# Loading x by blocks of 32 rows to 128 partitions instead of by column strips to 32

## The chip, the core and the metric

The kernel runs on one core of a Trainium2 chip. A core has a matrix engine (PE, with its weight loads PEld), a vector engine (DVE), a scalar engine (ACT), a general one (POOL) and SyncE (SP), which here issues nearly all transfers between the device's memory (HBM) and the on-chip memory of 128 partitions (SBUF). The transfers are carried out by sixteen DMA engines. The metric is device time in microseconds (us) of one execution.

## The reference

One graph layer over 128 graphs of 128 nodes with 768 features and 12 heads of 64, all in float32:

```
h = relu(layernorm(x))                     # per node, over 768 features
q, k, v = h @ Wq + bq, h @ Wk + bk, h @ Wv + bv
scores = q k^T / 8 + beta * adj            # per head
scores = where(adj > 0, scores, -9e15)
out = x + softmax(scores) v                # heads put side by side
```

So each graph needs its x twice: once normalized and turned for the products, and once as it is for the last sum.

## The kernel before

The graphs go in 32 groups G of four; a group is two pairs (r = 0, 1) of graphs. The weights stay the same for all groups. The three products q, k and v of a group are done in three slices, `qk0`, `v`, `qk1` (half of the columns of q and k, all of v, the other half). From group 1 on, each slice is a product of a 2 x 3 by a 3 x 3 table of blocks in 15 block products (`PRODUCTS`) instead of 18, and each block product is done in 7 zones instead of 8. The combined weight blocks (T, 128 x 896 values) are made once; eleven stay in SBUF and the other 34 of a group's 45 are kept in HBM and loaded anew for each group (`load_T`, L440) into a ring of five buffers (`RING`). A load of the ring is issued when the product that used the buffer before has ended. The products are `product`, L681: 7 zones by 2 halves, which the profile shows as 28 matmul records.

**x for the products.** The pair tile (`xp[G, r]`, made by `home_x`) holds x in a form of its own: partition a*32 + i, block m = 4g + b, 192 values: graph g of the pair, row 32b + i, features 192a to 192a + 191. There are two such pairs in a group but one buffer for both, so a pair is loaded when the pair before it was turned. ACT normalizes block by block in place (`norm`, L560; eight instructions of 128 x 192 per pair), DVE turns 32 x 32 squares (`to_hT`, L580), three times per pair, into the operands A. The scales and shifts of the norm come by another way: whole rows of x (`load_row`, L513) are summed by ACT, and the few numbers are written to HBM (`turn_out`, L539, "turned<-row") and read back by all partitions (`turn_in`, L543, "block<-turned").

**How x comes.** `load_x` issues a transfer for each a: source 32 rows i, 8 blocks (g, b), 192 values; destination 32 partitions with 8 x 192 values each. The four parts of a pair are issued at four places of the program.

**What sets the order.** In the groups from 1 on the order of all steps is written out: `TABLE` gives each step a time in units of a block product (45 to a group, counted from the group's start), and the steps are put into the program in the order of these times, between the block products. So the engines' queues, SP's among them, are in the order of the table. x of pair 0 is issued two groups ahead, in the `qk1` slice (times about -53 to -49, of which -45 is one group), among the loads of T for the next group's `qk0`; x of pair 1 one group ahead, at the end of `qk0` (times about -33 to -30), among the loads of T for `v`. SP is in order: a transfer that waits holds all behind it. The transfers take turns over eight semaphores, and each waits until the one that last used its semaphore has landed.

SP also loads x once more for the last sum (`load_xo`, L763), the adjacency (`load_adj`, L599) and sends the result (`send`, L908).

Of the kernel before, what the change touches and what calls it, by code (L numbers as in the profile page):

```python
# [20 lines left out]
GRP = 4  # L21
# [10 lines left out]
@with_exitstack  # L32
def kernel(
    ctx: ExitStack,
    tc: tile.TileContext,
    x: bass.AP,
    adj: bass.AP,
    wq: bass.AP,
    bq: bass.AP,
    wk: bass.AP,  # L40
    bk: bass.AP,
    wv: bass.AP,
    bv: bass.AP,
    beta: bass.AP,
    out: bass.AP,
):

    nc = tc.nc
    keep = ctx.enter_context(tc.tile_pool(name="keep", bufs=1))
    bad = keep.tile([1, 1], I32, name="bad")
    args = (x, adj, wq, bq, wk, bk, wv, bv, beta, out)
    direct(tc, *args, bad)
    again = nc.values_load(bad[0:1, 0:1])
    with tc.If(again > 0):
        general(tc, *args)  # L60
# [64 lines left out]
TABLE = (  # L125
    (-103.105, 'row', 0), (-86.74, 'row_stats', 0), (-85.688, 'row', 1), (-78.233, 'row_stats', 1),
    (-76.202, 'row', 2), (-71.584, 'row_stats', 2), (-67.928, 'row', 3), (-64.453, 'row_stats', 3),
    (-54.853, 'moments'), (-53.424, 'load_x', 0, (0,)), (-50.853, 'load_x', 0, (1,)), (-49.522, 'powers'),
    (-51.725, 'load_x', 0, (2,)), (-49.052, 'turn_out'), (-49.398, 'load_x', 0, (3,)), (-46.515, 'turn_in'),
    (-40.942, 'norm', 0, 2, 4), (-41.357, 'norm', 0, 0, 2), (-40.317, 'norm', 1, 2, 4), (-39.199, 'norm', 1, 0, 2),  # L130
    (-37.336, 'turn', 'A01'), (-34.768, 'turn', 'A02'), (-35.86, 'turn', 'A00'), (-33.123, 'load_x', 1, (0,)),
    (-32.146, 'load_x', 1, (1,)), (-30.708, 'load_x', 1, (2,)), (-32.534, 'load_x', 1, (3,)), (-24.763, 'inner', 'A00'),
    (-24.393, 'norm', 2, 0, 2), (-25.315, 'norm', 2, 2, 4), (-23.262, 'norm', 3, 2, 4), (-23.244, 'norm', 3, 0, 2),
    (-23.578, 'inner', 'A01'), (-20.844, 'adj'), (-18.417, 'inner', 'A02'), (-20.599, 'turn', 'A11'),
# [4 lines left out]
    (5.399, 'sum', 'S5'), (8.41, 'sum', 'S14'), (9.857, 'sum', 'S11'), (17.129, 'scores', 0, 2),  # L139
    (17.594, 'mask', 2), (18.011, 'exp', 2), (17.884, 'scores', 0, 1), (20.163, 'mask', 1),  # L140
    (23.187, 'exp', 1), (23.44, 'scores', 0, 0), (24.691, 'mask', 0), (26.808, 'xo', 2),
    (29.787, 'exp', 0), (33.304, 'attend', 2), (34.708, 'drain', 2), (38.169, 'recip', 2),
    (37.453, 'attend', 1), (40.226, 'divide', 2), (40.335, 'xo', 1), (40.001, 'drain', 1),
    (40.047, 'attend', 0), (42.314, 'xo', 0), (41.101, 'drain', 0), (41.291, 'recip', 1),
    (42.019, 'add', 2), (43.363, 'send', 2), (41.655, 'recip', 0), (47.272, 'xo', 5),
    (42.336, 'divide', 0), (46.026, 'divide', 1), (47.4, 'add', 1), (49.422, 'send', 1),
    (47.396, 'scores', 1, 2), (47.912, 'mask', 5), (47.949, 'scores', 1, 0), (49.895, 'add', 0),
    (49.151, 'mask', 3), (51.424, 'send', 0), (50.757, 'exp', 5), (51.214, 'scores', 1, 1),
    (51.428, 'mask', 4), (56.184, 'xo', 4), (50.986, 'exp', 3), (52.741, 'attend', 5),
    (53.334, 'drain', 5), (53.605, 'recip', 5), (54.069, 'divide', 5), (54.524, 'attend', 3),  # L150
    (55.36, 'drain', 3), (57.434, 'recip', 3), (54.287, 'xo', 3), (57.116, 'add', 5),
    (58.808, 'send', 5), (52.838, 'exp', 4), (58.432, 'divide', 3), (57.867, 'attend', 4),
    (58.283, 'drain', 4), (58.872, 'recip', 4), (61.984, 'divide', 4), (63.775, 'add', 3),
    (69.353, 'add', 4), (70.997, 'send', 4), (72.651, 'send', 3),
)
FIRST = (
# [70 lines left out]
def direct(ctx, tc, x, adj, wq, bq, wk, bk, wv, bv, beta, out, bad):  # L227
# [10 lines left out]
    nc = tc.nc  # L238
# [9 lines left out]
    SQ = 32  # L248
    NB = P // SQ
# [12 lines left out]
    xg, xp, A, full, wide, biasT, vt, qk = {}, {}, {}, {}, {}, {}, {}, {}  # L262
# [8 lines left out]
    def flat(lo, hi):  # L271
        return sbig[:, lo:hi]
# [7 lines left out]
    def home_x(G, r):  # L280
        if (G, r) in ((0, 0), (1, 1)):
            t = flat(2 * RAW, 2 * RAW + 2 * D).rearrange("p (m f) -> p m f", f=QD)
        else:
            t = work.tile([P, 2 * NB, QD], F32, tag="x", name=f"x_{G}_{r}", bufs=1)
        xp[G, r] = t
        for g in range(2):
            xg[G, 2 * r + g] = t[:, g * NB:(g + 1) * NB, :]
        return t

    def load_x(G, r, parts=range(NB)):  # L290
        if parts[0] == 0:
            home_x(G, r)
        src = x[G * GRP + 2 * r:G * GRP + 2 * r + 2].rearrange("g (b i) (a f) -> a i (g b) f", i=SQ, a=NB)
        for a in parts:
            nc.sync.dma_start(xp[G, r][a * SQ:(a + 1) * SQ], src[a])


# [144 lines left out]
    raw_qk0(0, (nc.sync, nc.scalar))  # L442
    raw_qk0(1)
    load_x(0, 1)
    raw_qk0(2)
    name_raw(0, qk0_raw)
# [130 lines left out]
    def to_hT(G, r, k):  # L577
        t = home_A(G, f"A{r}{k}")
        src = xp[G, r].rearrange("p m (c j) -> p c m j", c=NC)[:, 2 * k:2 * k + 2]
        return nc.vector.transpose(t.rearrange("p c (m i) -> p c m i", i=SQ), src)  # L580
# [178 lines left out]
    es, xo = {}, {}  # L759
# [432 lines left out]
    def then(at, f, *args):  # L1192
        todo.setdefault(at, []).append(lambda: f(*args))
# [83 lines left out]
    for r in range(2):  # L1277
        then(5, load_x, 1, r)
# [32 lines left out]
        then(n, step, 2 - (n > 8))  # L1311
    sums_at(1, ((12, "S1"), (13, "S9"), (14, "S10"), (15, "S2")))
    then(0, row_moments, 2)
    for a in range(NB):
        then((7 + a, "post"), load_x, 2, 0, (a,))
    then((14, "post"), load_row, 3, 0)
    then(12, homes.append, block(len(SPOT)))
    bias(1, 4, 6, 8)
    for n in range(2, RING):
# [4 lines left out]
        "scores": scores, "scores3": lambda G, u, js: [scores(G, u, j) for j in js], "mask": mask, "exp": expo, "xo": load_xo, "attend": attend, "drain": drain, "recip": recip,  # L1324
        "divide": divide, "add": add, "send": send, "sum": sum_acts, "norm": norm, "inner": inner,
        "turn": lambda G, name: to_hT(G, int(name[1]), int(name[2])), "bias1": bias_turn, "square": bias_square,
        "bias2": bias_mask, "bias3": bias_sum, "load_x": load_x, "row": load_row, "row_stats": row_stats,
        "moments": moments, "powers": powers, "turn_out": turn_out, "turn_in": turn_in, "adj": add_raw,
        "halve": lambda G: halve_bias(), "scores_half": scores_half, "attend_half": attend_first, "out_half": out_half,
    }  # L1330
# [19 lines left out]
    while events:  # L1350
        _, _, f, args = heapq.heappop(events)
# [149 lines left out]
```

## Time and profile before

| | us |
|---|---|
| median of 3 runs | 2677.48 (2674.48 to 2677.64) |
| the profiled execution | 2675.62 |
| its span, first to last instruction | 2673.7 |
| PE busy / DVE / ACT / POOL | 2645.9 / 2165.9 / 1754.7 / 2089.9 |
| HBM read / written | 647.99 MB / 66.05 MB |

A page of the profile gives busy times, the DMA queues, the waits and the chain of work that ended last; a view by window gives each engine's busy time and the mean busy share of the sixteen DMA engines ("DMA share"); a timeline gives instructions in order of time, with the start in us, the duration in us, the engine, the line and "out<-in". "SPq" is SP's queue: the duration there is that of the issue, and "x3" means that rows are merged, with the waits between them. "Landing" is the time from an issue until all of the data is there. A row of waits reads: who waited, for whom, us in total, times, the longest.

### The profile page before, as it was taken

The page shows a single profiled execution, that of the slowest core. Times are in us where ns is not written, and L with a number is a line of the kernel's source. Part 1 is how long each engine was busy: PE and PEld are TensorE (multiplying, and loading weights), DVE is VectorE, ACT ScalarE, POOL GpSimd, SP SyncE. Part 2 cuts the span into 40 slices and gives each one's busy share as a digit, 9 for nine tenths or more (in the row PEclk, how much of TensorE's full clock was granted, in tenths as well). Part 3 has the DMA queues.
Part 4 walks back from the last instruction along what each step waited for, and adds up shares of the span by engine and source line. Part 5 has one row for each costly group of instructions (what it writes and reads, how often), then busy time and mean ns, then how long its engine had stood idle before and what let it go on. Part 6 is the DMA issues. An engine that isn't in the chain of part 4 may idle for free.

```text
span 2673.7 us, 121363 instructions
## 1 busy us (share of the span) xinstructions
PE 2645.9 (99%) x52041; PEld 2565.2 (96%) x52041; DVE 2165.9 (81%) x2702; ACT 1754.7 (66%) x4608; POOL 2089.9 (78%) x3043
## 2 busy tenths in 40 slices
PE   9999999999999999999999999999999999999998
PEld 8799999999999999999999999999999999999997
DVE  7878887878887778888788877888887888778876
ACT  2567766677766677666777666776667776667654
POOL 4877778877778877788777788777887777887774
PEclk9999999999999999999999999999999999999999
DMA  8888888888888988888888888889888888888875
GB/s 247 270 272 270 276 280 272 275 287 262 285 279 272 282 269 271 281 278 269 280 265 283 278 272 267 274 271 285 272 272 280 265 282 280 265 277 275 249 247 165
DMA packets 526964, 721.97 MB, mean 270 GB/s; under 512 B 105932, under 2 KB 370648, under 8 KB 526424
## 3 DMA queue, kind: packets, MB, share of 16 engines
q1 hardware_dynamic: 525776, 713.38, 84.4%
q8 instruction: 411, 6.73, 1.0%
q14 instruction: 129, 1.06, 0.1%
q10 hardware_dynamic: 648, 0.79, 0.1%
HBM read 647.99 MB, written 66.05 MB: 267 GB/s over the span
## 4 chain that ended last, share of the span: by engine, by line
PE 95%; DMA 3%; DVE 1%; issue 0%; SPq 0%; ACT 0%; ACTq 0%; DVEq 0%
PE pair L681 78%; PE pair L776 7%; PE pair L855 6%; PE pair L1048 3%; DMA T_qk<-kept_qk 2%; DMA sbig<-in_L_gnn_Wk_dram 0%; PE pair L1265 0%; DVE home L704 0%; PE pair L1053 0%; DMA x<-in_x_dram 0%; SPq L336 0%; PE pair L926 0%; SPq L908 0%; DVE e L789 0%; DVE st L464 0%
## 5 line engine op out<-in xcount | busy, mean ns | idle before, releaser
L704 DVE TENSOR_TENSOR home<-home,pair 128x896 f32<-128x896 f32 x836 | 880.8, 1077 | 225.5 <-PE pair L681 192.7
L681 PE MATMUL pair<-sbig,T_qk 128*64 128x128 f32 x13020 | 833.0, 274 | 9.2 <-DMA T_qk<-kept_qk 6.9
L681 PEld LDWEIGHTS pair<-sbig,T_qk 128*64 128x64 f32 x13020 | 711.6, 137 | 28.7 <-issue 16.5
L739 POOL TENSOR_TENSOR home<-home 128x256 f32<-128x256 f32 x308 | 263.5, 855 | 339.3 <-DVE home L704 339.0
L681 PE MATMUL pair<-A,T_qk 128*64 128x128 f32 x6944 | 446.0, 273 | 0.3 <-issue 0.3
L855 PE MATMUL pair<-v,e 128*64 128x65 f32 x6048 | 412.6, 221 | 0.7 <-issue 0.7
L681 PE MATMUL pair<-T_v,sbig 128*64 128x128 f32 x6944 | 404.1, 273 | 2.1 <-issue 1.5
L681 PEld LDWEIGHTS pair<-T_v,sbig 128*64 128x64 f32 x6944 | 382.2, 137 | 8.3 <-ACT e L836 5.0
L836 ACT ACTIVATE e<-e,sm 128x64 f32<-128x64 f32 x1512 | 381.7, 341 | 5.0 <-DVE sm L824 3.4
L681 PEld LDWEIGHTS pair<-A,T_qk 128*64 128x64 f32 x6944 | 384.0, 137 | 0.4 <-issue 0.4
L855 PEld LDWEIGHTS pair<-v,e 128*64 128x64 f32 x6048 | 370.7, 137 | 3.8 <-issue 0.8
L724 ACT ACTIVATE home<-pair 128x640 f32<-128x640 f32 x340 | 240.4, 707 | 189.0 <-PE pair L681 187.7
L681 PE MATMUL pair<-sbig,res_qk 128*64 128x128 f32 x4340 | 314.0, 273 | 0.3
L742 POOL TENSOR_TENSOR home<-home 128x256 f32<-128x256 f32 x308 | 264.3, 858 | 24.1
L885 ACT ACTIVATE sm<-pair,tiny 128x8 f32<-128x8 f32 x189 | 50.8, 269 | 338.4 <-PE pair L855 338.4
L789 DVE SCALAR_TENSOR_TENSOR e<-pair,biasT 128x1024 f32<-128x1024 f32 x189 | 229.3, 1213 | 34.1 <-PE pair L776 33.1
L740 POOL TENSOR_TENSOR home<-home 128x256 f32<-128x256 f32 x308 | 230.6, 749 | 24.1
L681 PEld LDWEIGHTS pair<-sbig,res_qk 128*64 128x64 f32 x4340 | 240.5, 137 | 1.4 <-DVE home L704 1.3
L560 ACT ACTIVATE x<-x,block 128x192 f32<-128x192 f32 x480 | 222.6, 540 | 0.0
L726 ACT ACTIVATE home<-pair,bqk 128x128 f32<-128x128 f32 x680 | 214.1, 377 | 0.0
L798 ACT ACTIVATE e<-e 128x1024 f32<-128x1024 f32 x189 | 196.1, 1055 | 20.3 <-DVE e L789 12.7
L741 POOL TENSOR_TENSOR home<-home 128x128 f32<-128x128 f32 x308 | 180.4, 586 | 24.2
(208 smaller groups left out, 4489.9 us busy)
## 6 DMA issues: line engine op xcount, KB each, us to landing
T_qk<-kept_qk SPq DMA_DIRECT2D x713, 448.0 KB, 4.7
T_v<-kept_v SPq DMA_DIRECT2D x341, 448.0 KB, 4.7
xo<-in_x_dram SPq DMA_DIRECT2D x190, 256.0 KB, 5.3
out_dram<-xo SPq DMA_DIRECT2D x189, 256.0 KB, 5.2
x<-in_x_dram SPq DMA_DIRECT2D x248, 192.0 KB, 7.6
sbig<-in_x_dram SPq DMA_DIRECT2D x116, 384.0 KB
kept_qk<-prep_qk SPq DMA_DIRECT2D x23, 448.0 KB, 2.8
adj<-in_adj_dram SPq DMA_DIRECT2D x128, 64.0 KB, 4.1
```

The costliest lines, as they stand in the source:

```text
L560: nc.scalar.activation(t, t, AF.Relu, bias=shift[G, n], scale=rstd[G, n])
L681: nc.tensor.matmul(p[q:q + HD, at, :], lhs[:, q:q + HD], rhs, start=(first and at % 4 == 0), stop=True, skip_group_check=True)
L704: nc.vector.tensor_tensor(t, t, p[:, 0:7], op)
L724: nc.scalar.activation(t[:, 0:5], p[:, 0:5], AF.Copy, scale=float(sign))
L726: nc.scalar.activation(t[:, at], p[:, at], AF.Identity, bias=bqk[:, of, oc:oc + 1], scale=float(sign))
L739: e.tensor_tensor(t[:, 1:4:2], t[:, 1:4:2], twice(5), ALU.add)
L740: e.tensor_tensor(t[:, 2:5:2], t[:, 2:5:2], twice(1), ALU.add)
L742: e.tensor_tensor(t[:, 0:7:6], t[:, 0:7:6], twice(2), ALU.add)
L789: nc.vector.scalar_tensor_tensor(e[:, :, at], ps[:, :, at], SCORE_CAP * ISCALE, bias[:, :, at], op0=ALU.min, op1=ALU.add)
L798: nc.scalar.activation(e, e, AF.Exp, scale=1.0 / ISCALE)
L836: nc.scalar.activation(o[:, r, b, 0:HD], pa[:, r, b, 0:HD], AF.Copy, scale=t[:, 1, r, b:b + 1])
L855: nc.tensor.matmul(pa[q:q + HD, 2 * g + i, :], k[:, q:q + HD], vt[G, "v", r, h // 4][:, 4 * g + h % 4, :], start=True, stop=True, skip_gro ...
```

## The change

The transfers of a pair's x become eight, one for each graph g and block b of 32 rows (`load_piece`, m = 4g + b): source 96 KB of HBM in one piece (32 rows of 768 values), read as 4 strips a, 32 rows i and 192 values; destination block m of all 128 partitions. The table has two pieces at the place of each old part (0.02 and 0.32 behind it, in the order of time). The rest of the table has the same times and is only sorted. The three pairs that are loaded in the opening (pair 1 of group 0 and both of group 1, the last into a buffer of its own) still come by `load_x`. All but SP's queue keep their instructions and their order.

```diff
-    (-54.853, 'moments'), (-53.424, 'load_x', 0, (0,)), (-50.853, 'load_x', 0, (1,)), (-49.522, 'powers'),
+    (-54.853, 'moments'), (-53.404, 'piece', 0, 0), (-53.104, 'piece', 0, 1), (-51.705, 'piece', 0, 2),
...
-    def load_x(G, r, parts=range(NB)):
-        if parts[0] == 0:
+    def load_piece(G, r, m):
+
+        if not m:
             home_x(G, r)
+        g, b = m // NB, m % NB
+        nc.sync.dma_start(xp[G, r][:, m], x[G * GRP + 2 * r + g, b * SQ:(b + 1) * SQ].rearrange("i (a f) -> a i f", a=NB))
+
+    def load_x(G, r):
+        home_x(G, r)
         src = x[G * GRP + 2 * r:G * GRP + 2 * r + 2].rearrange("g (b i) (a f) -> a i (g b) f", i=SQ, a=NB)
-        for a in parts:
+        for a in range(NB):
             nc.sync.dma_start(xp[G, r][a * SQ:(a + 1) * SQ], src[a])
...
-    for a in range(NB):
-        then((7 + a, "post"), load_x, 2, 0, (a,))
+    for m in range(2 * NB):
+        then((7 + m // 2, "post"), load_piece, 2, 0, m)
```

On SP, x of pair 0 of group 9 (the names are tiles with their numbers, then the shape of the destination) stands before the change so:

```order
L295 DMA x_0_9848<-in_x_dram 32x8x192
L440 DMA T_qk_1_9867<-kept_qk_1_366 128x896
L440 DMA T_qk_0_9903<-kept_qk_0_360 128x896
L295 DMA x_0_9848<-in_x_dram 32x8x192 x2
L440 DMA T_qk_5_9943<-kept_qk_5_449 128x896
L763 DMA xo_1_9955<-in_x_dram 128x4x128
L295 DMA x_0_9848<-in_x_dram 32x8x192
L539 DMA turned_9962<-row_9_9957 4x32x8
L763 DMA xo_0_10025<-in_x_dram 128x4x128
```

and behind the change so (the same lines stand 8 further down in the file):

```order
L297 DMA x_0_9904<-in_x_dram 128x1x192 x2
L448 DMA T_qk_1_9924<-kept_qk_1_366 128x896
L448 DMA T_qk_0_9960<-kept_qk_0_360 128x896
L297 DMA x_0_9904<-in_x_dram 128x1x192 x4
L448 DMA T_qk_5_10002<-kept_qk_5_449 128x896
L771 DMA xo_1_10014<-in_x_dram 128x4x128
L297 DMA x_0_9904<-in_x_dram 128x1x192 x2
L547 DMA turned_10022<-row_9_10016 4x32x8
L771 DMA xo_0_10085<-in_x_dram 128x4x128
```

Each part has become two pieces at the same place. At the end of `qk0`, x of pair 1 of group 8 stands among the loads of T for `v`; before the change:

```order
L295 DMA x_1_9199<-in_x_dram 32x8x192 x3
L440 DMA T_v_9251<-kept_v_782 128x896
L513 DMA sbig<-in_x_dram 128x768
L908 DMA out_dram<-xo_5_8890 128x4x128
L440 DMA T_v_9282<-kept_v_743 128x896
L295 DMA x_1_9199<-in_x_dram 32x8x192
L440 DMA T_v_9300<-kept_v_656 128x896
```

and behind it:

```order
L297 DMA x_1_9251<-in_x_dram 128x1x192 x5
L448 DMA T_v_9305<-kept_v_782 128x896
L297 DMA x_1_9251<-in_x_dram 128x1x192
L521 DMA sbig<-in_x_dram 128x768
L916 DMA out_dram<-xo_5_8942 128x4x128
L448 DMA T_v_9337<-kept_v_743 128x896
L297 DMA x_1_9251<-in_x_dram 128x1x192 x2
L448 DMA T_v_9356<-kept_v_656 128x896
```

Here the sixth piece has come behind the first T, ahead of the row and the sent result.

More of the change, by code (lines that the diff above doesn't have):

```diff
@@ L127 @@
     (-76.202, 'row', 2), (-71.584, 'row_stats', 2), (-67.928, 'row', 3), (-64.453, 'row_stats', 3),
-    (-54.853, 'moments'), (-53.424, 'load_x', 0, (0,)), (-50.853, 'load_x', 0, (1,)), (-49.522, 'powers'),
-    (-51.725, 'load_x', 0, (2,)), (-49.052, 'turn_out'), (-49.398, 'load_x', 0, (3,)), (-46.515, 'turn_in'),
-    (-40.942, 'norm', 0, 2, 4), (-41.357, 'norm', 0, 0, 2), (-40.317, 'norm', 1, 2, 4), (-39.199, 'norm', 1, 0, 2),
-    (-37.336, 'turn', 'A01'), (-34.768, 'turn', 'A02'), (-35.86, 'turn', 'A00'), (-33.123, 'load_x', 1, (0,)),
@@ L132 @@
-    (-32.146, 'load_x', 1, (1,)), (-30.708, 'load_x', 1, (2,)), (-32.534, 'load_x', 1, (3,)), (-24.763, 'inner', 'A00'),
-    (-24.393, 'norm', 2, 0, 2), (-25.315, 'norm', 2, 2, 4), (-23.262, 'norm', 3, 2, 4), (-23.244, 'norm', 3, 0, 2),
-    (-23.578, 'inner', 'A01'), (-20.844, 'adj'), (-18.417, 'inner', 'A02'), (-20.599, 'turn', 'A11'),
[3 rows of a table removed]
+    (-54.853, 'moments'), (-53.404, 'piece', 0, 0), (-53.104, 'piece', 0, 1), (-51.705, 'piece', 0, 2),
+    (-51.405, 'piece', 0, 3), (-50.833, 'piece', 0, 4), (-50.533, 'piece', 0, 5), (-49.522, 'powers'),
@@ new lines @@
+    (-49.378, 'piece', 0, 6), (-49.078, 'piece', 0, 7), (-49.052, 'turn_out'), (-46.515, 'turn_in'),
+    (-41.357, 'norm', 0, 0, 2), (-40.942, 'norm', 0, 2, 4), (-40.317, 'norm', 1, 2, 4), (-39.199, 'norm', 1, 0, 2),
+    (-37.336, 'turn', 'A01'), (-35.86, 'turn', 'A00'), (-34.768, 'turn', 'A02'), (-33.103, 'piece', 1, 0),
+    (-32.803, 'piece', 1, 1), (-32.514, 'piece', 1, 2), (-32.214, 'piece', 1, 3), (-32.126, 'piece', 1, 4),
+    (-31.826, 'piece', 1, 5), (-30.688, 'piece', 1, 6), (-30.388, 'piece', 1, 7), (-25.315, 'norm', 2, 2, 4),
@@ L138 @@
+    (-24.763, 'inner', 'A00'), (-24.393, 'norm', 2, 0, 2), (-23.578, 'inner', 'A01'), (-23.262, 'norm', 3, 2, 4),
+    (-23.244, 'norm', 3, 0, 2), (-20.844, 'adj'), (-20.599, 'turn', 'A11'), (-18.464, 'inner', 'A11'),
[3 rows of a table added]
     (-6.5, 'sum', 'S6'), (-3.644, 'sum', 'S10'), (1.532, 'sum', 'S0'), (3.671, 'sum', 'S7'),
     (5.399, 'sum', 'S5'), (8.41, 'sum', 'S14'), (9.857, 'sum', 'S11'), (17.129, 'scores', 0, 2),
-    (17.594, 'mask', 2), (18.011, 'exp', 2), (17.884, 'scores', 0, 1), (20.163, 'mask', 1),
+    (17.594, 'mask', 2), (17.884, 'scores', 0, 1), (18.011, 'exp', 2), (20.163, 'mask', 1),
@@ L141 @@
     (23.187, 'exp', 1), (23.44, 'scores', 0, 0), (24.691, 'mask', 0), (26.808, 'xo', 2),
[L142 to L152, printed above, removed]
@@ L153 @@
-    (58.283, 'drain', 4), (58.872, 'recip', 4), (61.984, 'divide', 4), (63.775, 'add', 3),
+    (29.787, 'exp', 0), (33.304, 'attend', 2), (34.708, 'drain', 2), (37.453, 'attend', 1),
+    (38.169, 'recip', 2), (40.001, 'drain', 1), (40.047, 'attend', 0), (40.226, 'divide', 2),
+    (40.335, 'xo', 1), (41.101, 'drain', 0), (41.291, 'recip', 1), (41.655, 'recip', 0),
+    (42.019, 'add', 2), (42.314, 'xo', 0), (42.336, 'divide', 0), (43.363, 'send', 2),
+    (46.026, 'divide', 1), (47.272, 'xo', 5), (47.396, 'scores', 1, 2), (47.4, 'add', 1),
@@ new lines @@
+    (47.912, 'mask', 5), (47.949, 'scores', 1, 0), (49.151, 'mask', 3), (49.422, 'send', 1),
+    (49.895, 'add', 0), (50.757, 'exp', 5), (50.986, 'exp', 3), (51.214, 'scores', 1, 1),
+    (51.424, 'send', 0), (51.428, 'mask', 4), (52.741, 'attend', 5), (52.838, 'exp', 4),
+    (53.334, 'drain', 5), (53.605, 'recip', 5), (54.069, 'divide', 5), (54.287, 'xo', 3),
+    (54.524, 'attend', 3), (55.36, 'drain', 3), (56.184, 'xo', 4), (57.116, 'add', 5),
+    (57.434, 'recip', 3), (57.867, 'attend', 4), (58.283, 'drain', 4), (58.432, 'divide', 3),
@@ L154 @@
+    (58.808, 'send', 5), (58.872, 'recip', 4), (61.984, 'divide', 4), (63.775, 'add', 3),
     (69.353, 'add', 4), (70.997, 'send', 4), (72.651, 'send', 3),
@@ L1326, in direct @@
         "turn": lambda G, name: to_hT(G, int(name[1]), int(name[2])), "bias1": bias_turn, "square": bias_square,
-        "bias2": bias_mask, "bias3": bias_sum, "load_x": load_x, "row": load_row, "row_stats": row_stats,
+        "bias2": bias_mask, "bias3": bias_sum, "piece": load_piece, "row": load_row, "row_stats": row_stats,
         "moments": moments, "powers": powers, "turn_out": turn_out, "turn_in": turn_in, "adj": add_raw,
```

6 rows, old and new, of the table TABLE are left out of this document.

## The prediction

> **What bounds the kernel now.** I read the page first, for the share of each engine; then the waits of PE; then the loads that PE waits for; then the queue that issues them, in the two stretches that the change touches.
>
> ```profile
> span 2673.7 us, 121363 instructions
> PE 2645.9 (99%) x52041; PEld 2565.2 (96%) x52041; DVE 2165.9 (81%) x2702; ACT 1754.7 (66%) x4608; POOL 2089.9 (78%) x3043
> ...
> q1 hardware_dynamic: 525776, 713.38, 84.4%
> ```
> ```profile
> PE pair L681 <- DMA T_qk<-kept_qk: 6.9, 9, 1.4
> ```
> ```profile
> L440 SPq DMA_DIRECT2D T_qk<-kept_qk x713: 319/320/3638, 101.0 to 2640.1; - x179
> ...
> DMA to landing us min/median/max: 3.1/4.7/8.7
> ```
>
> PE is busy 99% of the span: nothing can gain more than the 28 us that are left, and of these only 6.9 us are waits for weight blocks T, the one thing on PE's path that shares a resource with x. But the DMA engines are the second bound: the packets of queue q1 fill 84.4% of sixteen engines' whole span. PE hides the T stream because five buffers are loaded ahead; it stops hiding it when a load takes longer than the room between its issue and its product.
>
> The rows of one graph group in the middle (81 us long) show that room. First the DMA share of the group and of the stretches around the two loads of x (last but one column; the last is GB/s):
>
> ```profile
> 1171.00:1252.00 81.00, 81.00 (x1644) 79.23 (x1642) 66.14 (x80) 55.62 (x146) 65.35 (x95) 1.00 0.87 277
> 1174.00:1184.00 10.00, 10.00 (x202) 9.88 (x200) 9.08 (x12) 5.10 (x19) 9.37 (x13) 1.00 0.75 219
> 1184.00:1189.00 5.00, 5.00 (x102) 4.74 (x102) 4.90 (x6) 3.54 (x12) 4.61 (x7) 1.00 0.96 306
> 1208.00:1215.00 7.00, 7.00 (x148) 7.00 (x146) 6.25 (x10) 3.51 (x13) 6.45 (x10) 1.00 0.92 256
> 1215.00:1222.00 7.00, 7.00 (x159) 6.66 (x156) 2.82 (x5) 5.94 (x15) 6.37 (x11) 1.00 0.82 260
> ```
>
> Then what SP issues in the first stretch (x of pair 0, issued in qk1 among the loads for the next group's qk0), and the products of the loads of 1182.24, 1184.03 and the next (28 matmul records make a product, loads are used in the order of issue):
>
> ```profile
> 1173.91 0.92 SPq L295 DMA_DIRECT2D x<-in_x_dram  x2
> 1176.72 0.34 SPq L440 DMA_DIRECT2D T_qk<-kept_qk  x1
> 1177.11 0.43 SPq L763 DMA_DIRECT2D xo<-in_x_dram  x1
> 1177.59 1.43 SPq L295 DMA_DIRECT2D x<-in_x_dram  x1
> 1179.12 0.55 SPq L539 DMA_DIRECT2D turned<-row  x1
> 1179.71 0.48 SPq L763 DMA_DIRECT2D xo<-in_x_dram  x1
> 1182.24 0.34 SPq L440 DMA_DIRECT2D T_qk<-kept_qk  x1
> 1182.67 0.63 SPq L908 DMA_DIRECT2D out_dram<-xo  x1
> 1183.39 0.54 SPq L543 DMA_DIRECT2D block<-turned  x1
> 1184.03 1.69 SPq L440 DMA_DIRECT2D T_qk<-kept_qk  x2
> ```
> ```profile
> 1190.32 4.81 PE L681 MATMUL pair<-sbig,T_qk 128*64 128x128 f32 x84
> ```
>
> The second stretch (pair 1, issued at the end of qk0 among the loads for v), with the landing of the T issued at 1211.32, and the products of the loads of 1212.96 and 1214.86:
>
> ```profile
> 1207.82 0.43 SPq L763 DMA_DIRECT2D xo<-in_x_dram  x1
> 1208.35 2.53 SPq L295 DMA_DIRECT2D x<-in_x_dram  x3
> 1211.32 0.34 SPq L440 DMA_DIRECT2D T_v<-kept_v  x1
> ...
> 1212.96 0.33 SPq L440 DMA_DIRECT2D T_v<-kept_v  x1
> 1213.99 0.33 SPq L295 DMA_DIRECT2D x<-in_x_dram  x1
> 1214.86 6.61 SPq L440 DMA_DIRECT2D T_v<-kept_v  x2
> ```
> ```profile
> DMA to landing us min/median/max: 6.2/6.2/6.2
> ```
> ```profile
> 1225.52 3.23 PE L681 MATMUL pair<-T_v,sbig 128*64 128x128 f32 x56
> ```
>
> So the load of 1184.03 is used at about 1190.32 + 4.81/3 = 1191.9, 7.9 us after its issue; with the median landing of 4.7 it has 3.2 us to spare. The load of 1214.86 is used at 1225.52 + 3.23/2 = 1227.1, 12.3 us after its issue; in this crowded stretch a landing lies between the 6.2 shown and the maximum of 8.7, so it has 3.6 to 6.1 us to spare.
>
> **The change part by part.** *More instructions on SP.* 248 issues make 62 pairs of graphs; the two pairs of the opening are not changed, so 60 are, two in each of 30 groups. Four issues become eight. The price of a piece is read from the nearest form. A piece's source is 4 blocks of 32 rows and its destination 128 partitions; two transfers have a 4-by-32 form already:
>
> ```profile
> L539 SPq DMA_DIRECT2D turned<-row x30: 541/553/648, 100.3 to 2484.4; - x30
> L543 SPq DMA_DIRECT2D block<-turned x30: 536/541/657, 112.5 to 2489.5; - x30
> L295 SPq DMA_DIRECT2D x<-in_x_dram x248: 312/444/2062, 10.8 to 2519.8; - x124
> ```
>
> They cost 0.54 us, the old x parts 0.44. With the 0.05 us between two issues a pair takes 8 x 0.59 = 4.7 us instead of 4 x 0.49 = 2.0. This is hidden: in the first stretch four pieces (2.4 us) stand where two parts (0.92) stood, from 1173.91, and end at 1176.3, ahead of the T of 1176.72, which waits for PE to free its buffer; in the second five pieces (3.0 us) replace three parts (2.53) ahead of the T of 1211.32. If that cover went, a T would be issued 0.5 us later, against 3 us to spare. I take 0.
>
> *The same bytes on fewer DMA engines.* This decides. The bytes and packets stay (768-byte runs, 1,024 to a pair). What no row of before shows is over how many of the sixteen engines a piece is spread, and that is the unknown with ends far apart: sixteen costs nothing, four costs what follows. I take four, by the two transfers above, the only ones of this form in a group: the trace's landing records, of which no view prints a row, hold sixteen updates for a T and five for each of these two (four engines that report and one remainder), and their issue price sets them apart from all the rest too.
>
> [...]
>
> The price: q1's packets took 0.844 x 16 x 2673.7 = 36,100 engine-us for 713.38 MB, 50.6 us per MB. A pair's x is 4 parts of 32 x 8 x 192 values of 4 bytes, 0.786 MB, 39.8 engine-us: 2.5 us on each of sixteen engines, 9.95 us on each of four. Every T is spread over all the engines and has landed when its slowest part has, so behind a pair's x each T is late by up to 9.95 - 2.5 = 7.5 us, less the idle time that these four engines had.
> - First stretch: idle 0.25 x 10 + 0.04 x 5 = 2.7 us until the T of 1184.03 lands. 7.5 - 2.7 = 4.8 us late, 3.2 to spare: PE waits about 1.6 us.
> - Second: idle 0.08 x 7 + 0.18 x 7 = 1.8 us. 5.7 us late, 3.6 to 6.1 to spare: PE waits 0 to 2.1 us.
> - The balance of a group: the four engines are busy 0.87 x 81 = 70.5 us and get 2 x 7.5 = 15 more, 85.5 us. They cannot do this in 81: at least 4.5 us a group, if packets take as long as now, wherever PE then waits.
>
> The local walk gives 1.6 to 3.7 us a group, the balance 4.5. I take the balance: what the walk leaves undone is carried into the next stretch, and there are places with nothing to spare already. One of PE's nine waits for T, in another group, stands some 10 us behind the four transfers of adj, at the start of qk1:
>
> ```profile
> 986.15 2.46 SPq L599 DMA_DIRECT2D adj<-in_adj_dram  x4
> ```
> ```profile
> 998.29 1.75 PE L681 MATMUL pair<-sbig,T_qk 128*64 128x128 f32 x28 [1.03 <-DMA T_qk<-kept_qk]
> ```
>
> That gives 30 x 4.5 = 135 us. Below, 30 x 1.6 = 48 (only the first stretch waits). Above, both, since the balance supposes that the four engines never idle while PE's waits hold back the next loads: 4.5 + 3.7 = 8.2, or 246 us.
>
> *Finer dependencies, and eight in flight.* The normalization of a block (L560) now needs its piece alone and not all four parts; since PE's row of waits is about T, earlier data is taken to gain 0, and at most the 28 us. A later last piece (up to 7.5 us) can hold ACT, which is in order. SP's transfers carry eight semaphores in turn, so each is issued only when the eighth ahead of it has landed; with five pieces in a row the T of 1212.96 and of 1214.86 get pieces as their eighth ahead, and late pieces make them late. On the four engines a T would stand behind these pieces anyway, so neither is counted twice; both are reasons for the upper end.
>
> **The sum.** The profiled execution took 2675.6 us, 1.9 around its span; the median of the three runs is 2677.5. 2677.5 + 135 = 2812; the ends are 2677 + 48 = 2725 and 2677 + 246 = 2923.
>
> **The rivals.**
> - *Sixteen engines after all* (spread by the 128 partitions of the destination). For it: that the old parts and T have 128 or 32 rows outside and sixteen updates; against it: block, whose destination is 128 partitions too. Time 2677, within 0.2%.
> [...]
> - *Four engines, but hidden.* If packets on four engines take much less time than the average one (the other twelve being freer), the spare 3.2 and 3.6 us cover it: under 1.5 us a group, 2690 to 2720.
> - *Worse than the balance.* SP is in order, and block (1183.39) waits for turned, issued right behind the last pieces and with a quarter of the engines too; behind block stands the T of 1184.03. If turned lands 7.5 us later, the T is issued about as late: 5 us of PE for the first stretch instead of 1.6, and with the upper end of the second and ACT's late normalization about 10 us a group: 2977.
>
> **How the numbers follow.** Likeliest, 2725 to 2923: 0.70. Hidden: 0.10. Worse than 2923: 0.10. Sixteen engines: 0.07. Faster: 0.03. About 0.2% (5 us) is what a measurement here can tell from no change. Slower 0.90, same 0.07, faster 0.03. To leave out no more than 2 in 10, the range reaches from the middle of the hidden case, 2700, to the beginning of the worst, 2950: 0.70 and about half of each of these two.
>
> **What would show it.** Right: landings of x of 10 us and more; PE's wait for T, 6.9 us in all now, grows to over 50 us and stands in qk0 and in v, in each group; the DMA share of the span falls, as fewer bytes move per us, while PE waits; issue of a piece near 0.54 us. Wrong: landings of x as before with PE's waits unchanged (sixteen engines); PE held by ACT or by SP's block instead of T (the worse case); or no T wait while x lands late (hidden).

## The result

| | us, median | runs | ratio to before, 95% interval |
|---|---|---|---|
| before | 2677.56 (2674.48 to 2678.29) | 4 | |
| after | 2697.44 (2692.88 to 2703.89) | 4 | 1.0078 [1.0054, 1.0102] |

The changed kernel is slower by 20 us. I had forecast 2812, slower by 135, in a range from 2700 to 2950; the sign is right, the size is wrong, and the time lies below the range. Other chips ran the kernel before in up to 2685.6 us (median), so below each time is given as a ratio to the kernel before on the same chip.

### The profile page after: what moved, and what is told of

It is laid out like the page before. It is cut to its first block, busy times and chain, and to the rows that moved or that the text cites. A ratio compares the mean times of both kernels' runs of the same rounds, so it can differ in the third digit from the quotient of the medians.

```text
span 2691.1 us, 121337 instructions
## 1 busy us (share of the span) xinstructions
PE 2652.0 (99%) x52041; PEld 2566.1 (95%) x52041; DVE 2166.5 (81%) x2702; ACT 1755.3 (65%) x4608; POOL 2086.2 (78%) x3043
## 3 DMA queue, kind: packets, MB, share of 16 engines
q1 hardware_dynamic: 523856, 713.38, 81.2%
## 4 chain that ended last, share of the span: by engine, by line
PE 87%; DMA 6%; POOL 3%; DVE 2%; issue 1%; SPq 1%; ACT 1%; ACTq 0%; POOLq 0%; DVEq 0%
PE pair L689 74%; PE pair L863 6%; PE pair L784 6%; DMA T_qk<-kept_qk 4%; DVE home L712 1%; PE pair L1056 1%; DMA sbig<-in_x_dram 1%; DMA turned<-row 0%; POOL prep_qk L394 0%; DMA sbig<-in_L_gnn_Wv_dram 0%; DMA sbig<-in_L_gnn_Wk_dram 0%; SPq L344 0%; POOL prep_qk L393 0%; DVE prep_qk L411 0%; DMA kept_qk<-prep_qk 0%
## 5 line engine op out<-in xcount | busy, mean ns | idle before, releaser
L863 PE MATMUL pair<-v,e 128*64 128x65 f32 x6048 | 420.6, 221 | 0.7 <-issue 0.6
L689 PEld LDWEIGHTS pair<-A,T_qk 128*64 128x64 f32 x6944 | 392.9, 137 | 5.2 <-issue 4.9
L863 PEld LDWEIGHTS pair<-v,e 128*64 128x64 f32 x6048 | 380.7, 137 | 4.3 <-issue 1.1
L689 PEld LDWEIGHTS pair<-sbig,res_qk 128*64 128x64 f32 x4340 | 247.7, 137 | 0.6 <-issue 0.5
```

The source lines that it names most:

```text
L689: nc.tensor.matmul(p[q:q + HD, at, :], lhs[:, q:q + HD], rhs, start=(first and at % 4 == 0), stop=True, skip_group_check=True)
L863: nc.tensor.matmul(pa[q:q + HD, 2 * g + i, :], k[:, q:q + HD], vt[G, "v", r, h // 4][:, 4 * g + h % 4, :], start=True, stop=True, skip_gro ...
```

## The profile after

The page, on the changed kernel (the profiled execution took 2692.88 us, the lowest of the four):

```profile
span 2691.1 us, 121337 instructions
...
PE 2652.0 (99%) x52041; PEld 2566.1 (95%) x52041; DVE 2166.5 (81%) x2702; ACT 1755.3 (65%) x4608; POOL 2086.2 (78%) x3043
...
q1 hardware_dynamic: 523856, 713.38, 81.2%
```

Its row of PE's waits for T, and the row of the pieces' issues (ns, min/median/max):

```profile
PE pair L689 <- DMA T_qk<-kept_qk: 14.1, 17, 4.2
```
```profile
L297 SPq DMA_DIRECT2D x<-in_x_dram x480: 528/557/2854, 113.0 to 2541.2; - x160
```

A middle group by window (DMA share last but one), as for the kernel before:

```profile
1182.50:1263.50 81.00, 79.05 (x1600) 76.90 (x1598) 65.06 (x78) 54.31 (x143) 65.34 (x94) 1.00 0.83 268
```

Three things are to be seen. PE's busy time rose by 6.1 us and its idle time by 11.3 (27.8 to 39.1 of the span); 7.2 us of the latter are waits for T. The issue of a piece costs 0.557 us, as priced. And the same 713.38 MB took less packet time: 81.2% of sixteen engines' 2691.1 us is 34,960 engine-us (one engine for one us), where it had been 36,100. So the packets took less time. That contradicts an assumption of the largest term of the prediction, which kept them as they were.

Next, SP's timeline in the first stretch of that group, which answers to the rows of 1173.91 to 1184.03 before:

```profile
1185.43 2.34 SPq L297 DMA_DIRECT2D x<-in_x_dram  x4
1188.23 0.57 SPq L448 DMA_DIRECT2D T_qk<-kept_qk  x1
1188.85 0.43 SPq L771 DMA_DIRECT2D xo<-in_x_dram  x1
1189.32 2.08 SPq L297 DMA_DIRECT2D x<-in_x_dram  x2
1191.50 1.01 SPq L547 DMA_DIRECT2D turned<-row  x1
1192.56 1.69 SPq L771 DMA_DIRECT2D xo<-in_x_dram  x1
1194.35 0.68 SPq L448 DMA_DIRECT2D T_qk<-kept_qk  x1
1195.13 0.38 SPq L916 DMA_DIRECT2D out_dram<-xo  x1
1197.72 0.54 SPq L551 DMA_DIRECT2D block<-turned  x1
1198.35 2.02 SPq L448 DMA_DIRECT2D T_qk<-kept_qk  x4
```

Before, block was issued 0.09 us after the sent result (1183.39 after 1182.67 + 0.63). Now the sent result is through at 1195.51 and block comes at 1197.72: SP stood 2.2 us, and it stood for turned, whose data block reads: by the landing records block is issued 0.06 to 0.08 us after turned has landed in each of 26 groups, where before the change it was 0.15 to 1.65 us. The T behind block is issued 12.92 us after the first of the four pieces above (1185.43), where it had been 10.12 after the parts of 1173.91, and four T are issued in a row, since by then their buffers are free. PE does not wait at this example, but the room is smaller.

The same over 26 groups, as medians worked out from the issue and landing records (times after the second T ahead of the row of pieces, which is that of 1182.71 in this group; "spare" is from the landing of a T to its product; T4 and T6 are the first and third T that stand behind block in the first two columns):

| us | before | after |
|---|---|---|
| turned issued at | 7.00 | 8.78 |
| turned, issue to landing | 3.95 | 6.14 |
| SP's gap ahead of block | 0.09 | 2.04 |
| T4 issued at | 12.70 | 15.84 |
| spare of T4 | 2.56 | 1.34 |
| spare of T6 | 3.39 | 0.88 |

A spare of 0.9 in the median means that some groups have none. The starts of the products that use a T, paired by number between the two traces, say how much: over groups 3 to 28 the changed kernel falls back by 13.0 us, 11.1 of it at the products of the loads behind pair 0 (0.43 us a group). The products behind pair 1 fall back by 0.7 in all, though their spare shrank too, the least from 5.0 to 1.4 in the median; the place behind adj loses 2.2, and others give 1.1 back. Another 5.4 arise at the opening.

There the first group's pair comes in pieces among SP's other work. The changed kernel, SP and then PE:

```profile
112.95 2.26 SPq L297 DMA_DIRECT2D x<-in_x_dram  x4
115.26 0.51 SPq L771 DMA_DIRECT2D xo<-in_x_dram  x1
115.87 0.92 SPq L397 DMA_DIRECT2D kept_qk<-prep_qk  x1
116.84 5.02 SPq L297 DMA_DIRECT2D x<-in_x_dram  x4
121.95 1.60 SPq L771 DMA_DIRECT2D xo<-in_x_dram  x1
123.60 1.93 SPq L448 DMA_DIRECT2D T_qk<-kept_qk  x3
```
```profile
129.62 3.25 PE L689 MATMUL pair<-sbig,T_qk 128*64 128x128 f32 x28 [4.15 <-DMA T_qk<-kept_qk]
```

and before, where the second half of the pair took 1.10 us and the T came at 118.04:

```profile
116.27 1.10 SPq L295 DMA_DIRECT2D x<-in_x_dram  x2
117.47 0.53 SPq L763 DMA_DIRECT2D xo<-in_x_dram  x1
118.04 2.52 SPq L440 DMA_DIRECT2D T_qk<-kept_qk  x3
```

The group behind the opening falls back by 5.4 us in this trace. PE's wait is 4.15 of these, and PE is slow right behind it: the 28 matmul records above take 3.25 us, where three times as many take 5.13 before. The view by window gives the granted clock there (the third number from the end), 0.50; before the change it is 1.00 in the stretches from 120 to 135 us.

```profile
129.50:133.00 3.50, 3.38 (x32) 3.07 (x36) 0.00 (x0) 0.09 (x1) 0.00 (x0) 0.50 0.98 390
```

## The experiments

After these readings I held two theories against each other. **M**: pieces hold back turned, SP stands at block until turned has landed, and the T behind block are issued late. **Balance**, as predicted: four engines have too much to carry, wherever that shows.

### Is it the four engines, or the number of transfers?

Eight transfers at the pieces' places, each one strip of one graph, so that the outermost size is 32 again:

```diff
-        g, b = m // NB, m % NB
-        nc.sync.dma_start(xp[G, r][:, m], x[G * GRP + 2 * r + g, b * SQ:(b + 1) * SQ].rearrange("i (a f) -> a i f", a=NB))
+        a, g = m // 2, m % 2
+        src = x[G * GRP + 2 * r + g].rearrange("(b i) (a f) -> a i b f", i=SQ, a=NB)
+        nc.sync.dma_start(xp[G, r][a * SQ:(a + 1) * SQ, g * NB:(g + 1) * NB], src[a])
```

> Each of the eight transfers of a pair is now one strip a of one graph g: 32 rows by 4 blocks of 192 values to 32 partitions. Number of transfers (8), bytes (96 KB each), packets (768 bytes), places in the queue are those of the changed kernel; only the outermost size of the patterns is 32 again instead of 4. Theory A (the loss comes from the four engines that a piece is spread over): back to the kernel before, 2673 to 2683 us. Theory B (the loss comes from twice as many issues and turns of the semaphores on SP): stays at the changed kernel's 2693 to 2700 us.

Measured: 0.9981 [0.9966, 0.9996]. The loss is gone with as many issues and turns of the semaphores. SP's timeline of this kernel in a middle group:

```profile
1181.63 0.55 SPq L548 DMA_DIRECT2D turned<-row  x1
1182.22 0.48 SPq L772 DMA_DIRECT2D xo<-in_x_dram  x1
1184.39 0.35 SPq L449 DMA_DIRECT2D T_qk<-kept_qk  x1
1184.84 0.39 SPq L917 DMA_DIRECT2D out_dram<-xo  x1
1185.32 0.54 SPq L552 DMA_DIRECT2D block<-turned  x1
1185.95 3.34 SPq L449 DMA_DIRECT2D T_qk<-kept_qk  x3
```

Block follows the sent result without a gap, and the medians are those of before: turned takes 3.50 us, T4 is issued at 12.72 and has 2.61 us to spare. So the loss hangs on the way a piece is spread, not on the count. A strip differs from a piece in its engines and in its partitions (32, not 128); eight transfers to 128 partitions on sixteen engines were not run in the kernel. That a piece has four engines is borne out by the landing records, sixteen updates for a part or a strip and five for each of the 480 pieces of the changed kernel, one of them 0.42 us behind the end of the issue in the median and the other four at least 2.3 us after that one, and by the packet records (no view prints either): in the changed kernel 768-byte packets run four at a time in 47% of the time in which any of them runs, and over five at a time in 4%; before the change it is over five in 49%, and with the strips and before up to sixteen and more.

### Which pair, and the opening

Three kernels undo the change for some pairs, with the four old parts (`load_part`, the old source and destination) at their old places in the table.

```diff
-    for m in range(2 * NB):
-        then((7 + m // 2, "post"), load_piece, 2, 0, m)
+    for a in range(NB):
+        then((7 + a, "post"), load_part, 2, 0, a)
```

> Only the pair of group 2 that is loaded in the opening comes in the four old parts; all other 59 pairs in pieces. The traces show the first product's start past the opening some 5 us later in the changed kernel, with one wait of 4.2 us for a T. Theory A1 (the opening's wait is a loss of its own): 2697.4 - 5 = about 2692 us. Rival (what is lost in the opening is taken up by slack behind it, or the loss is spread evenly over 60 pairs): 2697, within 2 us.

Pair 1 in parts, pair 0 in pieces:

```diff
-    ... (-33.103, 'piece', 1, 0),
-    (-32.803, 'piece', 1, 1), (-32.514, 'piece', 1, 2), (-32.214, 'piece', 1, 3), (-32.126, 'piece', 1, 4),
-    (-31.826, 'piece', 1, 5), (-30.688, 'piece', 1, 6), (-30.388, 'piece', 1, 7), ...
+    (-33.123, 'part', 1, 0), (-32.146, 'part', 1, 1), (-30.708, 'part', 1, 2), (-32.534, 'part', 1, 3),
```

> Pieces for pair 0 of each group (and the opening), the four old parts for pair 1. Theory A2 (the loss in the groups stands behind pair 0, where SP's block waits for turned and holds T): almost all of it stays, 2694 to 2698 us. Rival (balance: each pair's 7.5 us on four engines counts alike): half of the groups' 15 us goes, 2688 to 2690 us.

And pair 0 in parts, pair 1 in pieces (the same edit for `'piece', 0` with the old times of pair 0):

> Pieces for pair 1 of each group (and the opening), the four old parts for pair 0. Theory A2 (the loss in the groups stands behind pair 0): only the opening's 5 us are left, 2681 to 2685 us. Rival (balance: each pair counts alike): 2688 to 2690 us.

| | ratio to before |
|---|---|
| opening in parts, all else in pieces | 1.0071 [1.0055, 1.0088] |
| pieces for pair 0 (and the opening) | 1.0098 [1.0085, 1.0111] |
| pieces for pair 1 (and the opening) | 1.0009 [0.9998, 1.0020] |

Pieces for pair 0 alone cost as much as pieces for both, or more; pieces for pair 1 cost nothing that can be told. Both fall outside the times that either theory named: pair 0 alone lies above the 2694 to 2698 us (about 1.006 to 1.008) of A2, which is M here, and pair 1 alone just below its 2681 to 2685 (about 1.001 to 1.003), which its interval reaches. The balance, by which each pair counts alike, would have had about 1.004 for both, so it doesn't explain the loss. PE's waits with pieces for pair 0 alone, and SP at block there, 2.09 us behind the end of the sent result:

```profile
PE pair L696 <- DMA T_qk<-kept_qk: 29.4, 28, 3.9
```
```profile
1206.20 0.39 SPq L923 DMA_DIRECT2D out_dram<-xo  x1
1208.68 0.55 SPq L558 DMA_DIRECT2D block<-turned  x1
1209.32 1.85 SPq L455 DMA_DIRECT2D T_qk<-kept_qk  x4
```

In the median the T behind block is issued at 15.91 there, as late as in the changed kernel, and has 0.49 us to spare. Why this kernel should be slower than the one with both pairs in pieces isn't settled; the intervals overlap, 1.0085 to 1.0102.

The opening couldn't be told from this: minus 5 us would be 1.0059, no gain 1.0078, and the interval holds both. It is taken up again below.

### Is it SP's stop at block?

Block, and with it SP's wait for turned, moved behind three of the T (I had expected five to pass):

```diff
-    ... (-46.515, 'turn_in'),
+    ... (-43.6, 'turn_in'),
```

(For group 2 the step is already in the opening and is left out of the table.)

> The changed kernel (1.0078 times the kernel before) with the step of block (the read back of the scales, which waits for turned) moved 2.9 block products later, from -46.515 to -43.6 in the table, so that some five more loads of T stand ahead of it on SP. Pieces stay on four engines, and turned stays behind them. Theory M (the loss is SP standing at block until the late turned has landed, and T issued behind it): most of the loss goes, ratio to the kernel before 1.000 to 1.003. Rival D (T lands late because its own parts on the four busy engines take longer): ratio stays at 1.006 to 1.008.

Turned ahead of the last two pieces, block at its place:

```diff
-    (-49.378, 'piece', 0, 6), (-49.078, 'piece', 0, 7), (-49.052, 'turn_out'), (-46.515, 'turn_in'),
+    (-49.052, 'turn_out'), (-49.04, 'piece', 0, 6), (-49.02, 'piece', 0, 7), (-46.515, 'turn_in'),
```

> The changed kernel with turned issued ahead of the last two pieces of pair 0 instead of behind them; block stays at its place. Theory M: turned lands about 2 us earlier, SP's stop at block of about 2 us goes, ratio 1.001 to 1.004. Rival D: the same bytes on the same engines in the same 10 us, ratio 1.006 to 1.008.

The control is the kernel before with the first of these moves:

> Control: the kernel before with the same move of block as in the experiment that moves it. In its trace SP waits 0.1 us at block and the loads of T behind it have 2.6 us to spare. Both theories: 0.999 to 1.001. If it is under 0.998, the move is a gain of its own and has to be taken off.

| | ratio to before | gap ahead of block | T4 issued at | spare of T4, T6 |
|---|---|---|---|---|
| after | 1.0078 [1.0054, 1.0102] | 2.04 | 15.84 | 1.34, 0.88 |
| after, block later | 1.0021 [1.0010, 1.0031] | 0.09 | 13.20 | 1.60, 2.47 |
| after, turned first | 1.0030 [1.0016, 1.0043] | 0.10 | 14.10 | 1.18, 2.00 |
| before, block later | 1.0008 [0.9998, 1.0019] | | | |

Either move takes the gap away and with it about two thirds of the loss; neither changes a byte, a packet or the number of engines. Block's move by itself is worth nothing on the kernel before (turned's was not run there). M holds, within its expected 1.000 to 1.003 and 1.001 to 1.004. With turned first block still comes 0.06 us after turned has landed in 17 of 26 groups, so turned is only just in time, and T4 is issued 1.4 us later than before the change; but SP goes straight on from the sent result to block:

```profile
1195.02 1.13 SPq L448 DMA_DIRECT2D T_qk<-kept_qk  x1
1196.25 0.39 SPq L916 DMA_DIRECT2D out_dram<-xo  x1
1196.73 0.54 SPq L551 DMA_DIRECT2D block<-turned  x1
1197.36 2.37 SPq L448 DMA_DIRECT2D T_qk<-kept_qk  x4
```

### What is left, and the opening again

Both moves and the opening in the old parts; later the same once more beside a version with the opening in pieces:

> The changed kernel with three mends together: the pair of the opening in the four old parts, turned ahead of the last two pieces, block 2.9 block products later. 59 pairs stay in pieces on four engines. If theory M and the opening are the whole loss: 0.999 to 1.001 of the kernel before. If the four engines cost something of their own (late T on busy engines): 1.0015 to 1.003, as where block alone is moved.

> Two of the three mends: turned ahead of the last two pieces and block later, the opening's pair still in pieces. If the opening's wait of 4.2 us is a loss of its own: 1.0015 to 1.0025 of the kernel before, and 0.0015 to 0.0025 over the version with all three mends beside it. If it is given back later: both alike, 0.999 to 1.001.

> All three mends once more, on the same chip as the version without the opening's: 0.999 to 1.001 of the kernel before, as first measured (1.000).

| | ratio to before |
|---|---|
| all three mends | 1.0000 [0.9985, 1.0014] |
| all three mends, second time | 1.0021 [1.0009, 1.0034] |
| without the opening's mend | 1.0022 [1.0007, 1.0036] |

The second time missed the expected 0.999 to 1.001 and lies in the range named for a cost of the four engines; the first time was within it. Beside each other, the opening in parts and in pieces are alike, but the intervals reach 0.0014 to either side, and 5 us are 0.0019: whether the opening's loss stays in the total isn't settled. All pieces but the opening's are on four engines in these kernels, and the whole loss left is 0 to 0.2%, about 6 us (under 10 by the intervals' ends), where the balance wanted 135.

The starts of the products, paired with those of the kernel before as above, tell where each kernel falls back (us, one trace each; the opening is the group behind it, the other two columns are groups 3 to 28):

| | opening | behind pair 0 | behind adj |
|---|---|---|---|
| after | 5.4 | 11.1 | 2.2 |
| opening in parts | -0.3 | 15.4 | 6.9 |
| pieces for pair 0 | 4.2 | 25.1 | 6.3 |
| pieces for pair 1 | 4.5 | 3.5 | 3.9 |
| block later | 5.3 | 5.5 | 10.2 |
| turned first | 4.4 | 3.4 | 3.5 |
| all three mends | 0.4 | 1.3 | 9.2 |
| all three, second time | 0.3 | 2.1 | 1.9 |
| without the opening's mend | 2.9 | 3.7 | 7.0 |
| strips | -0.9 | -0.1 | 2.8 |
| before, block later | -0.5 | 0.5 | 0.2 |

The loss behind pair 0 comes with the late block and for the most part goes with it, which is M again. What is left in these traces stands for the most part behind adj, where a T has 0.4 us to spare before the change already; two traces of the same kernel differ there by 7 us. Whether the last 0.1 to 0.2% is real, and why it arises behind adj, stays open.

### What the same bytes cost on four engines

The disputed price by itself, in a kernel that only moves x:

```diff
...
+    for phase in (strip, piece, column, strip, piece, column):
+        for n in range(64):
+            phase(n)
+        nc.vector.tensor_copy(o, t)
...
```

> No layer is computed here: only 96 KB transfers of x, 64 in a row of each of three forms, twice round, and then copies of what came to the output, so the time is not that of the task. All have packets of 768 bytes. Form 1: a strip to 32 partitions, 32 rows outermost. Form 2: a piece to 128 partitions, 4 strips outermost. Form 3: a column of one graph to 128 partitions, 128 rows outermost. In the changed kernel the mean packet of 768 bytes took 37 ns instead of 46. If a packet is short because it goes to one of 128 partitions: forms 2 and 3 near 37 ns, form 1 near 46. If it is short because only four are under way at a time: form 2 short, forms 1 and 3 long. Four engines: 64 pieces take 64 x 128 x 37 ns / 4 = 76 us at least, and the DMA share is about 0.25 in form 2; the other two forms are limited by the issue at 64 x 0.49 = 31 us.

By window, inside the piece phase, the strip phase and the column phase (DMA share last but one, GB/s last), and the issue rows of pieces and of strips:

```profile
39.00:105.00 66.00, 0.00 (x0) 0.00 (x0) 1.00 0.27 93
5.50:32.80 27.30, 0.00 (x0) 0.00 (x0) 1.00 0.76 203
111.00:139.50 28.50, 0.00 (x0) 0.00 (x0) 1.00 0.75 204
```
```profile
L60 SPq DMA_DIRECT2D xs<-in_x_dram x128: 531/984/1306, 34.9 to 239.9; - x128
```
```profile
L56 SPq DMA_DIRECT2D xs<-in_x_dram x128: 311/430/475, 0.7 to 171.4; - x128
```

Four engines move 93 GB/s, so a piece of 98,304 bytes takes 1.06 us and a pair 8.5, not 9.95. In packet time that is 0.27 x 16 / 93 GB/s = 46.5 engine-us per MB, against 0.76 x 16 / 203 = 59.9 for strips and 58.8 for columns, and 50.6 as the mean of all packets in the kernel before. By the packet records pieces take 36 ns a packet in the mean, the other two 43 to 45; in the kernel before the packets of x took 45.6. Columns go to 128 partitions like pieces and take nearly as long as strips: a packet isn't short because of where it goes. The median is 36 ns in all three forms, so it is the long packets that are missing with four engines, most likely because few are under way at a time; a piece also reads 96 KB of HBM in a row, which strips and columns don't, and no run parts the two. Four engines of sixteen are a share of 0.25, and the share is 0.27, so packet times overlap: 1.08 for each of the four. That is also why 64 pieces took 71 us and not the "76 us at least". Strips and columns are held by their issue here (64 x 0.48 = 31 us), so their GB/s are no limit of the engines.

### A version that beats both?

The strips were the candidate, with block later and again as they are:

> Eight strips of one graph and 32 partitions each (sixteen engines; 0.9981 of the kernel before) and block moved later as well. In the trace of the strips SP waits 0.1 us at block, so the move should add nothing: 0.997 to 0.9985. It is also the candidate that may beat both kernels.

> The eight strips on sixteen engines once more, beside the mended version on one chip, as the candidate to beat both kernels. First measured at 0.9981, with block later at 0.9990: expected 0.9975 to 0.9995. A ratio of 1.000 or more would say that there is no gain.

Measured: 0.9990 [0.9982, 0.9999], a little above what was expected, and 0.9988 [0.9976, 1.0001], after 0.9981 the first time. Eight strips beat the changed kernel clearly and the kernel before by 0.1 to 0.2%, which is below what I called measurable; I don't claim it as a gain.

## Why the prediction was wrong

- **The step that failed is the balance of a group**: "the four engines are busy 0.87 x 81 = 70.5 us and get 2 x 7.5 = 15 more, 85.5 us. They cannot do this in 81: at least 4.5 us a group, if packets take as long as now". Both the packet times and the limit in it are off. *The packet times*: in the changed kernel's group the share is 0.83, 67.2 us on each of sixteen engines. By the packet records the 2,048 packets of two pairs take 37.2 ns each, 76.2 engine-us, 4.8 of the 67.2; without them 62.4 are left, and the four engines add a quarter of the 76.2, 19.0: 81.5 us, not 85.5. Most of the difference lies in the other transfers (65.5 to 62.4). That x itself came out near its 19.9 is luck: the 50.6 us per MB were a mean of all packets, while those of x took 45.6 ns before the change, 59.4 us per MB. *The limit*: 81 us of packet times in 81 us don't fill an engine, since packet times overlap (1.08 above). The same transfers on the same engines in a group of the kernel with all three mends show it:

```profile
1177.00:1258.00 81.00, 80.88 (x1637) 78.89 (x1634) 66.09 (x79) 55.77 (x146) 65.25 (x94) 1.00 0.85 274
```

  By the same sum the four engines have 83 us of packet times in these 81, and PE is busy for 80.88. In place of the term's 4.5 us a group the runs showed 0.43, and it comes from SP's stop at block.
- **The lower end was the wrong kind of bound.** 2725 came from the first stretch with 1.6 us a group. That stretch is where the loss is, but T4 lost 1.2 us of its spare instead of 4.8, because T is not late by the whole backlog on the four engines: it is late by the lateness of its issue behind block, and its own landing was quicker there (T4 is issued 3.1 us later, lands in 3.66 us instead of 5.39, and so lands 1.4 us later). So PE waits only in groups without room.
- **The time fell to the rival "four engines, but hidden"** (2690 to 2720), to which I had given 0.10. Half of its mechanism is right: packets on four engines take less time (37.2 ns instead of 45.6), and the spare covers most of the rest.
- **The other half stood among the rivals too**, as "worse than the balance": "block (1183.39) waits for turned, issued right behind the last pieces". This is what happens. I had priced it with turned 7.5 us late and 10 us of PE a group; turned is issued 1.8 us later, lands 4.0 us later in all, block stops SP for 2.0, and the T is issued 3.1 us later against 2.6 to 3.4 of room. It costs under 0.5 us of PE.
- **Four engines** was right, and so the sixteen-engine rival fell; the number of transfers is free, as the strips show.
- **More instructions on SP**: the issue price was right (0.54 forecast, 0.557 measured), and so was the cover ahead of the T of 1176.72. What I left out is that issues of pieces, turned and xo behind the first four grow to 1 to 1.7 us (2.08 for two pieces, 1.01 for turned in the rows above). They don't wait there for the semaphore of the eighth transfer ahead: by the landing records no issue of either kernel starts earlier than 0.016 us behind the landing of that transfer, but at each of the 29 long issues of turned it had landed 1.6 to 2.8 us earlier. With the strips turned's issue costs 0.55 again. In the kernel that only moves x (above) pieces are issued one every 1.06 us, the time in which the four engines move one, so the long issue seems to be the four engines' pace; that is argued, not shown.
- **The second stretch** was forecast at 0 to 2.1 us and costs 0: the T there keep 1.4 us or more in the median.
- **The signs** that I named: PE's wait for T was to go over 50 us and is 14.1 (29.4 in the worst experiment); it stands in `qk0`, at the opening and behind adj, and not in `v`. The fall in the DMA share did come, but for the most part because packets became shorter, not because PE waited. Landings of 10 us and more did not come: by its place among the eight a piece lands in 4.4 to 7.0 us in the median, and none takes over 8.9. A whole pair takes 17.5 and 16.2 us (pair 0, pair 1) from its first issue to its last landing, against 14.4 and 12.6.
- **Not put down to anything**: of the 17.4 us by which the span grew, only 7.2 are waits for T in the view of waits, though the starts of the products put 5.4 at the opening and 11.1 behind pair 0. Of the 6.1 us by which PE's busy time grew, 2.4 arise in the group behind the opening, where the granted clock fell to 0.50; the rest belongs to no wait that a view names.

## What to carry to other kernels

When bytes are pressed onto fewer DMA engines, don't take a sum of packet times for a limit: here packets were shorter when fewer ran together, and packet times overlapped on an engine, so that a balance that came out 5% over full still fitted. Look instead for the small transfer that now stands behind the large ones, and for the in-order queue that waits for it: here a 4 KB write, issued behind eight pieces, landed 4 us later and held SP for 2 us in each group. (That it lands late because it shares the pieces' four engines is argued: the traces do not name the engine of a packet.) Moving that transfer ahead, or its reader back, in the order gave back most of the loss without touching the large transfers.

## What was not expected of the hardware

Packets of the same 768 bytes took 36 ns in the mean with four engines at work and 43 to 45 with sixteen, whether they went to 32 or to 128 partitions; inside the kernel 37.2 and 45.6. And the DMA share of four engines alone was 0.27, over 4/16: packet times overlap somewhat on an engine, so a share of packet times near 1 isn't yet a full engine. The issue of turned behind the pieces took 1.1 us in the median instead of 0.55, although its semaphore had been free for 1.6 us and more.
